# Denominators from a channel of ones, transposed weights on SyncE's queue, and stores, filter writes and mixing on GpSimd, in a two-layer attention and spectral-filter kernel

## The chip, the cores and the metric

The kernel runs on one core of one Trainium2 chip. The metric is device time in microseconds (us) of one launch. A core has five engines that each work through their own list of instructions in order: TensorE (PE; its weight loads are listed as PEld), VectorE (DVE), ScalarE (ACT), GpSimd (POOL) and SyncE (SP). Transfers (DMAs) are issued by SP, ACT or POOL.

## The reference

The input x has the shape (2, 128, 64, 64). Layer 0 is a group norm and a block with 7x7 neighbourhood attention in 4 heads; the change touches only its last piece, which makes the tokens. Layer 1 works on 4096 tokens of 128 channels per batch:

```python
t = _to_tokens(x)
t = t + _L1_attn_ref(_ln_t(t))      # softmax(q q^T / sqrt(128)), diagonal masked, times q
t = t + _L1_ffn_ref(_ln_t(t), sigma, phi, M_u, M_phi_plus, M_phi_minus, log_weights, gumbel)
x = _from_tokens(t, x)
```

`_ln_t` is a layer norm without scale or shift, so the 128 channels of every token `q` sum to zero. `_L1_ffn_ref` is a causal convolution over the sequence with 16 filters `phi`, once on `u` and once on `u` with alternating signs; each filter has its own 128x128 matrices `M_phi_plus[i, k]` and `M_phi_minus[i, k]`, scaled by `sigma ** 0.25`. To it come three lags `M_u[i]`. There are four branches `i`, with sequences of 4096, 2048, 1024 and 512 tokens, summed with the weights of a hard choice over four values. The kernel computes with mixed matrices, the sum over the branches of weight times matrix.

## The kernel before

Three stages follow one another in time. From 0 to about 347 us layer 0 runs in an order written out by hand. From there to about 1341 us the attention of layer 1 runs, batch 0 and then batch 1, with smaller work laid between its steps. From 1341 us to the end the convolution runs as bursts and projections on 32-row tiles (L1511, L1530), which read what the attention stage wrote to DRAM. In the attention stage the kernel emits instructions pair by pair and a scheduler sets each engine's order.

**Attention.** A batch is 8 chunks of 512 tokens. Because q q^T is symmetric, only the 36 pairs (a, c) with a <= c are scored: `weights` makes a quarter of a pair, a matmul of the channel-major tokens `cm` (L923, L933), then `exp` on ScalarE (L928, L940), whose `accum_out` also adds up a row's sum into `part`. Four quarters of a pair are four steps. In every step one matmul adds to `other`, the rows of chunk c (L1052), and others to `own`, the rows of chunk a, which needs the transposed weights (L987). For 27 of the 36 pairs, the far ones, the transpose goes by DRAM: `sent` writes the 128x2048 weights to `eb` from ScalarE's queue (1 MB), `moved` reads them back into `et` by four DMAs that change places of 32-blocks (L961), and `turned` transposes inside the blocks on VectorE (two of L970) and sums them into `part` (L972). The constants `MOVE, TURN, DELAY = 2, 5, 6` say how many steps after the last quarter these are emitted, the last of them for the own matmuls. There are two `et` and four `eb` buffers. The pair (6, 7) is turned by TensorE (`turned_here`), the blocks on the diagonal by TensorE and VectorE (L946 to L948). The sums of `other` and `own` gather in `xa` (L992, L994, L1069, L1071).

**After a chunk.** When `own` of chunk a is whole, `complete` calls `fill`, which queues the generator `after`: it transposes `xa` (L1089), sums `part` and takes the reciprocal (L1091, L1092), adds the attention to the residual tokens `tt` (L1094), makes a layer norm (L183, L184 on VectorE, a power on GpSimd at L174, L191 on VectorE), transposes the result to `zc`, and computes the forward transform of the chunk for the convolution: matmuls with `tr`, then `store`, in which ScalarE copies half of a result from PSUM (L1115), VectorE adds and subtracts it into `ub` (L1118, four buffers) and SP writes `ub` to `us` in DRAM (L1122, L1127). An `after` issues 16 such DMAs. There are 16 `after`s, 8 in each batch. `yield True` ends a step of the queued work; a plain `yield` ends the turn of the generator too.

**Other work laid between.** `filters` computes the transformed filters from `phi_pad`, with GpSimd adds (L1326, L1337), and writes them to `gs` in DRAM by 32 SP DMAs (L1302). `tokens(1)` makes the tokens of batch 1. `mixed` loads the branches' matrices one after another into `st` (two buffers, SP, L1250), multiplies the first by its weight (L1253) and adds the others (L1255), on VectorE. `filter_matrices` calls it for 4 groups of 4 filters, plus and minus, and after each group makes sums and differences times `sg` (L1266 to L1271, `mdiff`); it runs between 963 and 1080 us, in batch 1. `short_lags` are the three lags (matmul L1180, L1196). After `filter_matrices`, `blocks` loads the first `ct` from `gs` (L1413).

**Start of the convolution.** Its first inputs `ut` (L1492) are read from `us` and wait until all of `us` is written.

The steps of a pair are passed on so:

```python
while coming_ and coming_[0][0] + MOVE <= step:
    at, eb, a, c = coming_.pop(0)
    et = moved(eb)
    turns.append((at + TURN, et, a, c))
    late.extend((at + DELAY, a, c, et, t) for t in range(4))
```

Of the kernel before, what the change touches and what calls it, by code (L numbers as in the profile page):

```python
# [14 lines left out]
P = 128  # L15
# [8 lines left out]
MASKED = -1.0e30  # L24
MOVE, TURN, DELAY = 2, 5, 6

# [76 lines left out]
def kernel(  # L103
# [100 lines left out]
    def token_tiles(b, n0, pt):  # L204
        for j in range(4):
# [7 lines left out]
            )  # L213

    def tokens(b, bank):

        for n0 in range(0, NT, 4):
            pt = bank()
            token_tiles(b, n0, pt)
            nc.scalar.copy(tt[b][:, n0 : n0 + 4, :].rearrange("p j c -> p (j c)"), pt)  # L220
            yield
            stats = ln_statistics(tt[b][:, n0 : n0 + 4, :])
            yield
            ln_apply(tok[b][:, n0 : n0 + 4, :], tt[b][:, n0 : n0 + 4, :], stats)
            yield
            pt = bank()
            transposed(pt, tok[b][:, n0 : n0 + 4, :])
            nc.scalar.copy(cm[b][:, n0 * P : (n0 + 4) * P], pt)
            yield

# [4 lines left out]
    with l0a:  # L235
# [489 lines left out]
        @piece("k.cm")  # L725
        def _(t, b, g):
            nc.scalar.copy(cm[0][:, t["n0"] * P : (t["n0"] + 4) * P], t["kb"])


# [141 lines left out]
    with ap_:  # L871
# [24 lines left out]
        def attention(b, fill):  # L896
# [9 lines left out]

            part = sp.tile([P, NT, 9], F32, tag="part", name="part", bufs=1)
            nc.gpsimd.memset(part[:, :, 8:9], 0.0)
            pairs = [(a, c) for a in range(8) for c in range(a, 8)]
# [3 lines left out]
            def weights(a, c, k, left, halves):  # L913

                n = 4 * CHUNKS[a] + k
                lo = k * P if a == c else 0
                ps = bank()
                if k == 0:
                    halves.append(ep.tile([P, 2048], F32, tag="e", name="e"))
                eh = halves[0]  # L920
                keys = cm[b][:, chunk(c)]
                if far(a, c):
                    nc.tensor.matmul(  # L923
                        ps.rearrange("p (q t j) -> p q t j", q=4, t=4), lhsT=cm[b][:, n * P : (n + 1) * P],
                        rhs=keys.rearrange("p (t q j) -> p q t j", t=4, q=4), start=True, stop=True,
                    )
                    e = eh.rearrange("p (q k r) -> p k q r", q=4, k=4)[:, k]
                    nc.scalar.activation(  # L928
                        e, ps.rearrange("p (q r) -> p q r", q=4), AF.Exp, bias=0.0, scale=ASCALE,
                        accum_out=part[:, n, c : c + 1],  # L930
                    )
                    return e
                nc.tensor.matmul(  # L933
                    ps[:, lo:], lhsT=cm[b][:, n * P : (n + 1) * P], rhs=keys[:, lo:], start=True, stop=True
                )
                if a == c:
                    ks = slice(k * P, (k + 1) * P)
                    nc.vector.tensor_tensor(ps[:, ks], ps[:, ks], ndiag, ALU.add)
                e = eh[:, k * 512 : (k + 1) * 512]
                nc.scalar.activation(  # L940
                    e[:, lo:], ps[:, lo:], AF.Exp, bias=0.0, scale=ASCALE, accum_out=part[:, n, c : c + 1]
                )
                if lo:
                    pt = bank()
                    for j in range(k):
                        nc.tensor.transpose(pt[:, j * P : (j + 1) * P], left[j][:, lo : lo + P], ident)  # L946
                    nc.vector.tensor_copy(e[:, 0:lo], pt[:, 0:lo])
                    nc.vector.tensor_reduce(part[:, n, 8:9], e[:, 0:lo], AX.X, ALU.add)  # L948
                return e
# [7 lines left out]
            def moved(eb):  # L957

                et = ep.tile([P, 4, 512], F32, tag="et", name="et", bufs=2)
                for q in range(4):  # L960
                    nc.gpsimd.dma_start(  # L961
                        out=et[32 * q : 32 * q + 32], in_=eb[:, q].rearrange("(h p) r -> p h r", h=4)
                    )
                return et

            def turned(et, a, c):

                for q in (0, 2):
                    flat = et[:, q : q + 2].rearrange("p q r -> p (q r)")
                    nc.vector.transpose(flat, flat)  # L970
                n0 = 4 * CHUNKS[c]
                nc.vector.tensor_reduce(  # L972
                    part[:, n0 : n0 + 4, a], et.rearrange("p q (k t i) -> p t (q k) i", k=4, t=4), AX.XY, ALU.add
                )

            def turned_here(et, es, a, c, m):
# [4 lines left out]
                n = 4 * CHUNKS[c] + m  # L981
                nc.scalar.activation(
                    et[:, m], pt, AF.Identity, bias=0.0, scale=1.0, accum_out=part[:, n, a : a + 1]
                )

            def onto(own, n, out_, e, first, last):
                nc.tensor.matmul(out_, lhsT=tok[b][:, n, :], rhs=e, start=first, stop=last, skip_group_check=True)  # L987

            def complete(a, own):
# [3 lines left out]
                else:  # L993
                    nc.vector.tensor_copy(xs, own)  # L994
                fill(CHUNKS[a], part)

# [23 lines left out]
            def pass_on(n):  # L1020

                while coming_ and coming_[0][0] + MOVE <= step:
                    at, eb, a, c = coming_.pop(0)
                    et = moved(eb)
                    turns.append((at + TURN, et, a, c))
                    late.extend((at + DELAY, a, c, et, t) for t in range(4))
                while turns and turns[0][0] <= step:
                    turned(*turns.pop(0)[1:])
                while n and late and late[0][0] <= step:
# [7 lines left out]
            for i, (a, c) in enumerate(pairs):  # L1037
# [6 lines left out]
                for j in range(4):  # L1044
# [11 lines left out]
                    if a != c and not far(a, c):  # L1056
                        if j == 0:
                            here = ep.tile([P, 4, 512], F32, tag="et", name="et", bufs=2)
                        turned_here(here, es, a, c, j)
                        late.append((step + 1, a, c, here, j))  # L1060
# [20 lines left out]

        def after(b, c, part):

            n0 = 4 * c
            par, hf = divmod(c, 4)
# [4 lines left out]
            rden = sp.tile([P, 4], F32, tag="rden", name="rden")  # L1090
            nc.vector.tensor_reduce(rden, part[:, n0 : n0 + 4, :], AX.X, ALU.add)  # L1091
            nc.vector.reciprocal(rden, rden)  # L1092
            for j in range(4):
                nc.vector.scalar_tensor_tensor(  # L1094
                    tt[b][:, n0 + j, :], pt[:, j * P : (j + 1) * P], rden[:, j : j + 1], tt[b][:, n0 + j, :],
                    ALU.mult, ALU.add,
                )
            yield
            borrowed = b == 1 and spare not in ([], [None])
            z = spare.pop() if borrowed else sp.tile([P, 4, P], F32, tag="z4", name="z4")  # L1100
            layernorm(z, tt[b][:, n0 : n0 + 4, :])
            yield
# [8 lines left out]
            def store(pu, n, r0, m, ri):  # L1111

                for s in range(2):
                    half = sp.tile([P, 256], F32, tag="uo", name="uo", bufs=2)
                    nc.scalar.copy(half[:, 0:n], pu[s][:, n : 2 * n])  # L1115
                    ub = sp.tile([P, 2, 256], F32, tag="ub", name="ub", bufs=4)
                    for sgn, op in enumerate((ALU.add, ALU.subtract)):
                        nc.vector.tensor_tensor(ub[:, sgn, 0:n], pu[s][:, 0:n], half[:, 0:n], op)  # L1118
                    for sgn in range(2):
                        to = us[r0 : r0 + m, sgn, :, 2 * hh + s, 2 * fp : 2 * fp + 2, b, par, :]  # L1120
                        if ri is not None:
                            nc.sync.dma_start(  # L1122
                                out=to[:, ri], in_=ub[:, sgn, :].rearrange("p (f d) -> p f d", d=P)
                            )
                            continue
                        for f in range(2):
                            nc.sync.dma_start(  # L1127
                                out=to[:, :, f].rearrange("k i d -> i k d"), in_=ub[64 * f : 64 * f + 64, sgn, 0:P]
# [116 lines left out]
        def mixed(dst, src):  # L1245
            dst2 = dst.rearrange("p k e -> p (k e)")
            for i in range(NBR):
# [26 lines left out]
        def filters():  # L1274
# [22 lines left out]
            def store(src, r0, n, ri, s, i, o):  # L1297
# [3 lines left out]
                )  # L1301
                nc.sync.dma_start(out=to, in_=src)  # L1302

# [43 lines left out]
        def filler(b, steps, kept=None):  # L1347

            urgent, done = [], []

            def fill(c=None, part=None):
                if c is not None:
                    done.append(c)
                    urgent.append(after(b, c, part))
                    if len(done) % 4 == 0:
# [446 lines left out]
```

## Time and profile before

| | value |
|---|---|
| median of 3 runs | 2115.12 us (2111.28 to 2119.82) |
| profiled execution | 2113.34 us |
| its span | 2111.6 us |
| granted TensorE clock, mean | 0.969 |
| DMA `et<-eb`, issue to landing | 5.6 us (median of 216) |
| `us<-ub` | 128 DMAs of 128 KB and 128 smaller ones |

The page names an instruction by its source line, engine, operation and tiles. Busy time is the sum of the durations of a group; the idle time beside it is the time the engine stood just before such an instruction, with what ended it. A wait that the page gives to one engine on another ends with the named instruction. All durations come from the one profiled execution; its span is 1.7 us shorter than its time. The windows cut the span into stretches and give each engine's busy time in them, with the number of its instructions.

### The profile page before, as it was taken

Reading aid. Unit: us, or ns where it says so; the run is one execution under the profiler, and the core shown is the slowest. Engines: PE = TensorE matmul, PEld = TensorE weight load, DVE = VectorE, ACT = ScalarE, POOL = GpSimd, SP = SyncE. Lnnn points to the kernel's source line nnn. Section 1 sums busy time; section 2 is a strip of 40 time slices with the busy share of each in tenths; the row PEclk is TensorE's granted clock in tenths of the full one; section 3 lists DMA queues with packets and bytes.
Section 4 is the critical chain, followed back from the end, with each engine's and each line's share of the span. In section 5 each row is a group of like instructions: output and inputs, shape, how many; then the busy total and the mean of one; then the engine's idle time right before and its main releaser. Section 6 shows DMA issues by size and latency. Waiting matters only on the chain.

```text
span 2111.6 us, 51431 instructions
## 1 busy us (share of the span) xinstructions
PE 1942.4 (92%) x20504; PEld 1356.1 (64%) x20504; DVE 1112.5 (53%) x3172; ACT 735.7 (35%) x1990; POOL 592.0 (28%) x996
## 2 busy tenths in 40 slices
PE   6899998977999999997689989899999999999998
PEld 4577775433444444443234444599999899999987
DVE  5799986644755565554665657433333334333332
ACT  3789985212233223222022222222222222222222
POOL 3367876424321111111111110022222112222211
PEclk9999999998999999998889999999999999999999
DMA  4222222565565542648665562222222123222211
GB/s 151 60 61 60 62 61 62 161 157 172 147 204 164 162 127 78 177 117 239 143 177 160 149 181 72 82 67 66 69 67 67 48 55 101 67 67 67 66 47 42
DMA packets 264558, 226.01 MB, mean 107 GB/s; under 512 B 122607, under 2 KB 241535, under 8 KB 256896
## 3 DMA queue, kind: packets, MB, share of 16 engines
q1 hardware_dynamic: 238338, 105.95, 18.7%
q0 software_dynamic: 17856, 58.73, 12.3%
q10 hardware_dynamic: 8126, 58.04, 6.9%
q8 instruction: 163, 2.67, 0.6%
q14 instruction: 75, 0.61, 0.1%
HBM read 131.40 MB, written 91.25 MB: 105 GB/s over the span
## 4 chain that ended last, share of the span: by engine, by line
PE 57%; DMA 9%; DVE 7%; POOL 2%; issue 2%; SPq 1%; ACT 1%; DVEq 0%; POOLq 0%; ACTq 0%
PE acc L1530 27%; PE own L987 8%; PE pc L1511 7%; PE other L1052 5%; PE bank L923 4%; DMA us<-ub 4%; DMA et<-eb 2%; PE bank L933 2%; DVE et L970 1%; DMA st<-in_m_minus_dram 1%; PE bank L202 1%; DMA st<-in_m_plus_dram 1%; PE bank L1180 1%; PE pc L1569 1%; POOL ln_rs L174 1%
## 5 line engine op out<-in xcount | busy, mean ns | idle before, releaser
L1516 DVE COPY y<-pc 128x512 f32<-128x512 f32 x320 | 206.2, 686 | 349.0 <-PE pc L1511 348.6
L1530 PE MATMUL acc<-y,mpl 32*128 32x256 f32 x5120 | 325.4, 380 | 0.8 <-DVE af L1540 0.8
L1530 PE MATMUL acc<-y,mmi 32*128 32x256 f32 x5120 | 316.5, 375 | 0.0
L1516 ACT COPY y<-pc 128x512 f32<-128x512 f32 x320 | 172.1, 589 | 397.2 <-PE pc L1511 380.6
L1530 PEld LDWEIGHTS acc<-y,mpl 32*128 32x128 f32 x5120 | 290.5, 186 | 8.2 <-DVE af L1540 1.3
L1530 PEld LDWEIGHTS acc<-y,mmi 32*128 32x128 f32 x5120 | 290.9, 185 | 3.9
L928 ACT ACTIVATE e<-bank 128x512 f32<-128x512 f32 x216 | 129.3, 599 | 411.9 <-PE bank L923 395.2
L1052 PE MATMUL other<-e,tok 128*128 128x512 f32 x448 | 232.4, 621 | 30.0 <-DVE xa L1069 13.3
L987 PE MATMUL own<-et,tok 128*128 128x512 f32 x448 | 213.7, 616 | 36.3 <-DVE et L970 36.1
L961 POOL DMA_DIRECT2D et<-eb x216 | 119.3, 558 | 415.4 <-DMA eb<-e 143.1
L923 PE MATMUL bank<-cm 128*128 128x512 f32 x432 | 222.8, 612 | 9.2 <-DVE ub L1118 8.9
L1511 PE MATMUL pc<-ct,ut 32*128 32x256 f32 x2560 | 213.1, 377 | 4.2 <-DMA ut<-us 2.3
L1541 POOL TENSOR_TENSOR af<-af 128x512 f32<-128x512 f32 x39 | 49.7, 1275 | 590.3 <-DVE af L1540 504.3
L987 PEld LDWEIGHTS own<-et,tok 128*128 128x128 f32 x448 | 86.5, 197 | 148.8 <-issue 98.5
L1511 PEld LDWEIGHTS pc<-ct,ut 32*128 32x128 f32 x2560 | 173.0, 186 | 10.4 <-DVE y L1516 3.9
L1052 PEld LDWEIGHTS other<-e,tok 128*128 128x128 f32 x448 | 84.1, 197 | 132.5 <-issue 112.5
L970 DVE STREAM_TRANSPOSE et<-et 128x1024 f32<-128x1024 f32 x108 | 128.0, 1220 | 27.3 <-DMA et<-eb 27.2
L923 PEld LDWEIGHTS bank<-cm 128*128 128x128 f32 x432 | 76.7, 195 | 84.3 <-issue 69.5
L972 DVE TENSOR_REDUCE part<-et 128x4 f32<-128x2048 f32 x54 | 123.2, 2282 | 1.1
L541 ACT ACTIVATE p<-p,mn 128x196 f32<-128x196 f32 x256 | 114.4, 449 | 12.9 <-DVE mn L531 12.3
L1118 DVE TENSOR_TENSOR ub<-bank,uo 128x256 f32<-128x256 f32 (+1 forms) x192 | 60.6, 372 | 110.5 <-DMA us<-ub 45.7
L174 POOL TENSOR_TENSOR ln_rs<-ln_rs,mhalf 128x4 f32<-128x4 f32 x24 | 24.7, 1030 | 289.5 <-DVE ln_rs L173 245.5
(264 smaller groups left out, 2672.5 us busy)
## 6 DMA issues: line engine op xcount, KB each, us to landing
eb<-e ACTq DMA_DIRECT2D x54, 1024.0 KB
et<-eb POOLq DMA_DIRECT2D x216, 256.0 KB, 5.6
ut<-us SPq DMA_DIRECT2D x160, 128.0 KB
us<-ub SPq DMA_DIRECT2D x128, 128.0 KB
ct<-gs SPq DMA_DIRECT2D x320, 40.0 KB
vw<-vd SPq DMA_DIRECT2D x256, 49.0 KB
ct<-gs SPq DMA_DIRECT2D x320, 32.0 KB
vd<-v SPq DMA_DIRECT2D x128, 32.0 KB
```

Source lines behind the costliest of these rows:

```text
L541: nc.scalar.activation(p, p, AF.Exp, bias=t[name + "mn"][:, h : h + 1], scale=-1.0, accum_out=t["den"][:, u, h : h + 1],)
L923: nc.tensor.matmul(ps.rearrange("p (q t j) -> p q t j", q=4, t=4), lhsT=cm[b][:, n * P : (n + 1) * P], rhs=keys.rearrange("p (t q j) -> p ...
L928: nc.scalar.activation(e, ps.rearrange("p (q r) -> p q r", q=4), AF.Exp, bias=0.0, scale=ASCALE, accum_out=part[:, n, c : c + 1],)
L961: nc.gpsimd.dma_start(out=et[32 * q : 32 * q + 32], in_=eb[:, q].rearrange("(h p) r -> p h r", h=4))
L970: nc.vector.transpose(flat, flat)
L972: nc.vector.tensor_reduce(part[:, n0 : n0 + 4, a], et.rearrange("p q (k t i) -> p t (q k) i", k=4, t=4), AX.XY, ALU.add)
L987: nc.tensor.matmul(out_, lhsT=tok[b][:, n, :], rhs=e, start=first, stop=last, skip_group_check=True)
L1052: nc.tensor.matmul(turn(other, "p (q r) -> p q r"), lhsT=tok[b][:, n, :], rhs=es[j], start=(j == 0), stop=(j == 3),)
L1118: nc.vector.tensor_tensor(ub[:, sgn, 0:n], pu[s][:, 0:n], half[:, 0:n], op)
L1511: nc.tensor.matmul(pcs[j].rearrange("p (g o c) -> p o g c", g=4, o=2)[:, :, at], lhsT=ut[rows_, par, :], rhs=cv_[rows_], start=True, stop= ...
L1516: (nc.scalar.copy if j % 2 else nc.vector.tensor_copy)(y[:, :, :, 4 * kl + j, :], pcs[j].rearrange("p (g x k) -> p k g x", g=4, k=KF))
L1530: nc.tensor.matmul(acc[j][:, 0:256], lhsT=(mmi if l else mpl)[rows_, k, :], rhs=y[rows_, k, 2 * l : 2 * l + 2].rearrange("p s n x -> p (s ...
```

## The change

1. Channel 127 of the value tokens `tok` is set to one after `cm` has been made (`count`), so channel 127 of `own` and `other` is the denominator. The sums into `part` (the `accum_out` of L928, L940, L982, the reductions L948, L972, L1091) are gone. `after` takes the reciprocal of channel 127 and rebuilds the true channel 127 as minus the sum of the other 127.
2. `MOVE, TURN, DELAY` become 3, 7, 8; the DMAs of `moved` are issued by SP; the transposes of `turned` and the own matmuls keep their program order. The copy of `turned_here` goes from ScalarE to VectorE.
3. `store`: ScalarE copies both halves of a result to SBUF, GpSimd adds and subtracts, and GpSimd issues the `us` DMAs.
4. The `gs` writes are issued by GpSimd.
5. `mixed` runs on GpSimd: a multiply in place and an add where there was one instruction.
6. `after` has two more `yield True`, at its start and between the statistics and the application of the layer norm.

```diff
-MOVE, TURN, DELAY = 2, 5, 6
+MOVE, TURN, DELAY = 3, 7, 8
...
+    def count(b, n0):
+        nc.gpsimd.memset(tok[b][:, n0 : n0 + 4, P - 1 : P], 1.0)
...
             nc.scalar.copy(cm[b][:, n0 * P : (n0 + 4) * P], pt)
+            count(b, n0)
...
             nc.scalar.copy(cm[0][:, t["n0"] * P : (t["n0"] + 4) * P], t["kb"])
+            count(0, t["n0"])
...
-            part = sp.tile([P, NT, 9], F32, tag="part", name="part", bufs=1)
-            nc.gpsimd.memset(part[:, :, 8:9], 0.0)
...
-                        e, ps.rearrange("p (q r) -> p q r", q=4), AF.Exp, bias=0.0, scale=ASCALE,
-                        accum_out=part[:, n, c : c + 1],
+                        e, ps.rearrange("p (q r) -> p q r", q=4), AF.Exp, bias=0.0, scale=ASCALE
...
-                nc.vector.tensor_reduce(part[:, n, 8:9], e[:, 0:lo], AX.X, ALU.add)
...
-                    nc.gpsimd.dma_start(
+                    nc.sync.dma_start(
                         out=et[32 * q : 32 * q + 32], in_=eb[:, q].rearrange("(h p) r -> p h r", h=4)
                     )
...
-            def turned(et, a, c):
+            def turned(et):
                 for q in (0, 2):
                     flat = et[:, q : q + 2].rearrange("p q r -> p (q r)")
-                    nc.vector.transpose(flat, flat)
-                n0 = 4 * CHUNKS[c]
-                nc.vector.tensor_reduce(
-                    part[:, n0 : n0 + 4, a], et.rearrange("p q (k t i) -> p t (q k) i", k=4, t=4), AX.XY, ALU.add
-                )
+                    tc.keep_in_program_order(nc.vector.transpose(flat, flat))
...
-                nc.scalar.activation(
-                    et[:, m], pt, AF.Identity, bias=0.0, scale=1.0, accum_out=part[:, n, a : a + 1]
-                )
+                nc.vector.tensor_copy(et[:, m], pt)
...
+                tc.keep_in_program_order(
+                    nc.tensor.matmul(out_, lhsT=tok[b][:, n, :], rhs=e, start=first, stop=last, skip_group_check=True)
+                )
-                nc.tensor.matmul(out_, lhsT=tok[b][:, n, :], rhs=e, start=first, stop=last, skip_group_check=True)
...
-        def after(b, c, part):
+        def after(b, c):
+            yield True
...
-            nc.vector.tensor_reduce(rden, part[:, n0 : n0 + 4, :], AX.X, ALU.add)
-            nc.vector.reciprocal(rden, rden)
+            kept_, out_ = tt[b][:, n0 : n0 + 4, :], pt.rearrange("p (j d) -> p j d", d=P)
+            nc.vector.reciprocal(rden, out_[:, :, P - 1])
+            rest = sp.tile([P, 4], F32, tag="rest", name="rest")
+            nc.vector.tensor_reduce(rest, out_[:, :, 0 : P - 1], AX.X, ALU.add)
             for j in range(4):
                 nc.vector.scalar_tensor_tensor(
-                    tt[b][:, n0 + j, :], pt[:, j * P : (j + 1) * P], rden[:, j : j + 1], tt[b][:, n0 + j, :],
+                    kept_[:, j, 0 : P - 1], out_[:, j, 0 : P - 1], rden[:, j : j + 1], kept_[:, j, 0 : P - 1],
                     ALU.mult, ALU.add,
                 )
+            nc.vector.tensor_tensor(rest, rest, rden, ALU.mult)
+            nc.vector.tensor_tensor(kept_[:, :, P - 1], kept_[:, :, P - 1], rest, ALU.subtract)
...
-            layernorm(z, tt[b][:, n0 : n0 + 4, :])
+            stats = ln_statistics(kept_)
+            yield True
+            ln_apply(z, kept_, stats)
...
-                    half = sp.tile([P, 256], F32, tag="uo", name="uo", bufs=2)
-                    nc.scalar.copy(half[:, 0:n], pu[s][:, n : 2 * n])
+                    both = sp.tile([P, 512], F32, tag="uo", name="uo", bufs=2)
+                    nc.scalar.copy(both[:, 0 : 2 * n], pu[s][:, 0 : 2 * n])
                     ub = sp.tile([P, 2, 256], F32, tag="ub", name="ub", bufs=4)
                     for sgn, op in enumerate((ALU.add, ALU.subtract)):
-                        nc.vector.tensor_tensor(ub[:, sgn, 0:n], pu[s][:, 0:n], half[:, 0:n], op)
+                        nc.gpsimd.tensor_tensor(ub[:, sgn, 0:n], both[:, 0:n], both[:, n : 2 * n], op)
...
-                            nc.sync.dma_start(
+                            nc.gpsimd.dma_start(
                                 out=to[:, ri], in_=ub[:, sgn, :].rearrange("p (f d) -> p f d", d=P)
...
-                            nc.sync.dma_start(
+                            nc.gpsimd.dma_start(
                                 out=to[:, :, f].rearrange("k i d -> i k d"), in_=ub[64 * f : 64 * f + 64, sgn, 0:P]
...
-                    nc.vector.tensor_scalar(dst2, st2, wt[:, 0:1], None, ALU.mult)
+                    nc.gpsimd.tensor_scalar(dst2, st2, wt[:, 0:1], None, ALU.mult)
                 else:
-                    nc.vector.scalar_tensor_tensor(dst2, st2, wt[:, i : i + 1], dst2, ALU.mult, ALU.add)
+                    nc.gpsimd.tensor_scalar(st2, st2, wt[:, i : i + 1], None, ALU.mult)
+                    nc.gpsimd.tensor_tensor(dst2, dst2, st2, ALU.add)
...
-                nc.sync.dma_start(out=to, in_=src)
+                nc.gpsimd.dma_start(out=to, in_=src)
```

More of the change, by code (lines that the diff above doesn't have):

```diff
@@ L940, in weights @@
                 nc.scalar.activation(
-                    e[:, lo:], ps[:, lo:], AF.Exp, bias=0.0, scale=ASCALE, accum_out=part[:, n, c : c + 1]
+                    e[:, lo:], ps[:, lo:], AF.Exp, bias=0.0, scale=ASCALE
                 )
@@ L964, in moved, with turned_here @@
                 return et
-            def turned(et, a, c):
+            def turned(et):
                 for q in (0, 2):
                     flat = et[:, q : q + 2].rearrange("p q r -> p (q r)")
-                    nc.vector.transpose(flat, flat)
-                n0 = 4 * CHUNKS[c]
-                nc.vector.tensor_reduce(
-                    part[:, n0 : n0 + 4, a], et.rearrange("p q (k t i) -> p t (q k) i", k=4, t=4), AX.XY, ALU.add
-                )
-            def turned_here(et, es, a, c, m):
+                    tc.keep_in_program_order(nc.vector.transpose(flat, flat))
+            def turned_here(et, es, m):
                 pt = bank()
@@ L980, in turned_here, with onto @@
                     nc.tensor.transpose(pt[:, k * P : (k + 1) * P], es[k][:, m * P : (m + 1) * P], ident)
-                n = 4 * CHUNKS[c] + m
-                nc.scalar.activation(
-                    et[:, m], pt, AF.Identity, bias=0.0, scale=1.0, accum_out=part[:, n, a : a + 1]
-                )
-            def onto(own, n, out_, e, first, last):
-                nc.tensor.matmul(out_, lhsT=tok[b][:, n, :], rhs=e, start=first, stop=last, skip_group_check=True)
+                nc.vector.tensor_copy(et[:, m], pt)
+            def onto(own, n, out_, e, first, last):
+                tc.keep_in_program_order(
+                    nc.tensor.matmul(out_, lhsT=tok[b][:, n, :], rhs=e, start=first, stop=last, skip_group_check=True)
+                )
             def complete(a, own):
@@ L994, in complete @@
                     nc.vector.tensor_copy(xs, own)
-                fill(CHUNKS[a], part)
+                fill(CHUNKS[a])
             def pair_onto(own, a, c, et, t):
@@ L1024, in pass_on @@
                     et = moved(eb)
-                    turns.append((at + TURN, et, a, c))
+                    turns.append((at + TURN, et))
                     late.extend((at + DELAY, a, c, et, t) for t in range(4))
                 while turns and turns[0][0] <= step:
-                    turned(*turns.pop(0)[1:])
+                    turned(turns.pop(0)[1])
                 while n and late and late[0][0] <= step:
@@ L1058, in attention @@
                             here = ep.tile([P, 4, 512], F32, tag="et", name="et", bufs=2)
-                        turned_here(here, es, a, c, j)
+                        turned_here(here, es, j)
                         late.append((step + 1, a, c, here, j))
@@ L1349, in filler, with fill @@
             urgent, done = [], []
-            def fill(c=None, part=None):
+            def fill(c=None):
                 if c is not None:
                     done.append(c)
-                    urgent.append(after(b, c, part))
+                    urgent.append(after(b, c))
                     if len(done) % 4 == 0:
```

## The prediction

> **What bounds the kernel now.** I read the page's shares and slices first, then busy time by stage, then what TensorE waits for, then the cost groups, and last the timeline of the last stores. The shares, and two rows of the slices:
>
> ```profile
> PE 1942.4 (92%) x20504; PEld 1356.1 (64%) x20504; DVE 1112.5 (53%) x3172; ACT 735.7 (35%) x1990; POOL 592.0 (28%) x996
> ...
> POOL 3367876424321111111111110022222112222211
> PEclk9999999998999999998889999999999999999999
> ```
>
> TensorE is busy 92% of the span; no other engine is over 53%. A slice is 2111.6/40 = 52.8 us. POOL stands at one tenth through slices 13 to 24, the attention: it has room. The same by stage (columns: window, length, busy us and count of PE, PEld, DVE, ACT, POOL, clock, DMA share, GB/s):
>
> ```profile
> 600.00:700.00 100.00, 95.06 (x277) 43.29 (x276) 62.79 (x121) 27.72 (x82) 20.48 (x34) 1.00 0.60 172
> ...
> 1000.00:1100.00 100.00, 70.10 (x172) 29.99 (x173) 66.67 (x128) 15.09 (x45) 11.95 (x21) 0.83 0.62 165
> ...
> 1350.00:2112.00 762.00, 746.49 (x13236) 722.04 (x13232) 260.45 (x464) 210.99 (x424) 165.75 (x390) 0.99 0.24 64
> ```
>
> The last 762 us, the spectral stage, have TensorE full and are not touched. The edits lie in 347 to 1341 us. There the windows give idle PE time of 59.7 us (347 to 950), 40.6 us (963 to 1080, where the filters of the branches are mixed, clock 0.81), 16.3 us (1080 to 1297) and 5.1 us (1297 to 1341). What PE waited for in 347 to 1341 (total, times, longest):
>
> ```profile
> PE own L987 <- DVE et L970: 36.1, 12, 12.8
> PE other L1052 <- DVE xa L1069: 13.3, 7, 7.4
> PE other L1052 <- DVE rden L1092: 9.1, 1, 9.1
> PE bank L923 <- DVE ub L1118: 8.9, 5, 3.9
> ...
> PE bank L946 <- DVE ub L1118: 7.4, 2, 3.9
> PE bank L1315 <- DVE ub L1118: 5.4, 1, 5.4
> ...
> PE bank L202 <- DVE ub L1118: 4.4, 2, 2.3
> ```
>
> So VectorE is named nearly always, though it is little over half busy: it works in order, and stands at one instruction while others are ready. Which instruction, the groups say (busy, mean ns | idle before, releaser):
>
> ```profile
> L961 POOL DMA_DIRECT2D et<-eb x216 | 119.3, 558 | 415.4 <-DMA eb<-e 143.1
> L1541 POOL TENSOR_TENSOR af<-af 128x512 f32<-128x512 f32 x39 | 49.7, 1275 | 590.3 <-DVE af L1540 504.3
> ...
> L970 DVE STREAM_TRANSPOSE et<-et 128x1024 f32<-128x1024 f32 x108 | 128.0, 1220 | 27.3 <-DMA et<-eb 27.2
> L972 DVE TENSOR_REDUCE part<-et 128x4 f32<-128x2048 f32 x54 | 123.2, 2282 | 1.1
> L1118 DVE TENSOR_TENSOR ub<-bank,uo 128x256 f32<-128x256 f32 (+1 forms) x192 | 60.6, 372 | 110.5 <-DMA us<-ub 45.7
> ```
>
> VectorE idles 110 us ahead of the stores' adds (L1118), 45.7 of it until a `us` transfer has given a `ub` buffer back. The end of the stage on SP's queue:
>
> ```profile
> 1326.03 4.09 SPq L1122 DMA_DIRECT2D us<-ub  x8
> 1330.21 4.43 SPq L1127 DMA_DIRECT2D us<-ub  x8
> 1338.65 2.24 SPq L1492 DMA_DIRECT2D ut<-us  x5
> ```
>
> The spectral stage's first load waits until every `us` store has landed, 4 us after the last issue: the stores of the last `after` are on the path.
>
> **What the Trainium skill says.** "GPSIMD Engine Reference", Performance versus the Vector engine: an elementwise add of two tensors takes GpSimd about twice as long as VectorE (1.96). The trace agrees: 1275 ns against 685 (L1069) at 128x512. "DMA: Bandwidth & Descriptors", Anatomy of one DMA: a semaphore wait of a transfer is held on the issuing sequencer. The trace agrees: POOL's `et` issues waited 143.1 us for `eb`; after the change SP waits so, with all behind it. The same page, Issuing engines are not separate DMA queues: another issuer saves sequencer time only. I take it so: `et` keeps its 5.6 us to land. The same page, SWDGE vs HWDGE vs iDMA: GpSimd computes descriptors in software. How long it takes for `us` stores in 512-byte runs no row shows; 558 ns for an `et` DMA in 2 KB runs is the nearest.
>
> **Part 1, the denominators.** Gone from VectorE: L972 123.2, L948 48 x 0.41 = 19.7, L1091 2.9 us. Added: one reduce of 128x508 an `after`, 16 x 0.6 = 10 (L972 is 1.1 ns an element), 32 tiny ones at 0.17 = 5, the turned copies of pair (6,7), 8 x 0.69 = 5.5. ScalarE loses 56 us of accumulator reads (42.0 and 14.1), which were not on the path. The memsets, 16 at some 0.2 us, lie in idle POOL.
>
> **Part 2, the way of `et`.** POOL loses 119.3 us of issue, SP gains them. After the score e leaves, `eb` takes 9 us, four issues 2.2, landing 5.6, two transposes 2.4: 19 us unhindered, up to 23 in the chain. A step is a quarter of a pair, 288 in both batches; PE's 859 busy us between 347 and 1341 make it 3.0 us. DELAY was 6 steps = 18 us, late by 1 to 5; with 8 it is 24. The two `et` buffers are held from step 3 to 12, 9 steps, where two buffers and a pair every 4 steps give 8: so `moved` also waits for the own matmuls of the pair two before, which end in step 3; some 5 steps = 15 us are left for the 10.2 of issue, landing and turn. That fits while SP has nothing else ahead; what does stand behind SP's wait there, `st` and `ct` loads, counts in part 5.
>
> **Part 3, the stores on POOL.** One `after` costs there 8 x 0.723 (L1326, 128x256) + 4 x 0.452 (L1546, 128x128) + 16 x 0.55 = 16.4 us; 16 of them 262 us. At twice the descriptor work of an issue (0.84) it would be 21; below 0.45, SP's fastest, nothing speaks for it: 15. VectorE loses 60.6 us, and above all the standing for `us`. ScalarE's copies grow from 0.34 to 0.60: 64 x 0.26 = 17 us beside PE. POOL meets `ub` itself: four buffers at 2.55 us are 10.2 us, over the 7.5 a `us` store takes, so it hardly stands. Behind a block of stores POOL holds the next layernorm's power (L174), and with it VectorE's z and PE's z transposes, by up to 16 us. The `after`s lie 35, 20 and 22 us apart at the batch boundary: 16.4 fits, and PE has scores to do meanwhile.
>
> **The gain of parts 1 to 3** outside mixing and end: the four `ub` waits 26.1; of L970's 36.1 the 9.7 outside 963 to 1080 (26.4 inside); of the waits for xa, z and tok (some 20 outside mixing) I credit 9, since VectorE's queue is shorter. The rden wait (9.1) stays: VectorE stands there for a filter load. 45 us. Bounds: 26 if only `ub` goes; 65 if most of the 76 us of idle goes with clock recovered.
>
> **Part 4, gs.** 32 issues x 0.55 = 18 us on POOL, between its own adds there: the filter stage has POOL 47 us; nothing to +8, I take 4.
>
> **Part 5, mixing on POOL.** Eight blocks of four loads, in pairs. VectorE did a load in 0.75 us, waiting 2.9 to 7 for it. POOL: 1.5 (128x512 by a scalar, L647 to L1337: 1.49 to 1.57) for the first, 1.5 + 1.28 for each other: 2 x 1.5 + 6 x 2.8 = 19.7 us a group, and with two `st` buffers and 3.4 us a load, walked by hand, 27.4 for the first group and 29.7 for each other: 117 us. Beside the 20 `ct` loads that share SP, 125 to 130. What hangs on it: in the program's order on VectorE the turns of pairs 11, 12, 13 of batch 1 follow the second, third and fourth mdiff (which need POOL's result), and on SP the `et` loads of pair 13 stand behind the 31st `st` load, which waits for POOL to free `st`. PE's own matmuls of 11 to 13 wait on all that. Before, from the stage's first z transposes (951.5) to the end of pair 13's own (1071.6) were 120 us. After: 13 + 127 + 10 = 150, less 4 of work that PE does in it: +26. Bounds: +5 (loads overlap fully, 4 x 19.7 = 79, PE then bound as before) and +50.
>
> **Part 6, the end.** Three `after`s come at 1297.7, 1302 and 1306. POOL issues in the order stores 6, power 7, stores 7, power 8, stores 8 (L174 is 1.0 us, and 4.4 us from the power's start through z, transposes and matmul to the next store). So 3 x 16.4 + 2 x 4.4 + 4 landing = 62 us from 1297.7, where before it was 40.7: +21; and those stores start about 7 us later against PE's work, as POOL still serves the one before: +28. Cover: lag matmuls (L1180) only, which PE has done by then. Bounds +12 and +40.
>
> **Sum.** -45 + 4 + 26 + 28 = +13 us on the profiled 2113.3: 2126. The median of the runs shown is 1.8 over the profiled time: 2128.
>
> **Rivals.** *Faster: VectorE's relief is worth more and the new prices hide.* For: VectorE is named in nearly all waits of PE; POOL's mean load after is only 450 of 994 us. Against: both prices stand in one engine's order. -55 + 5 + 10 = -40: 2075. *Much slower: GpSimd decides.* One mechanism: it builds descriptors for 512-byte runs at 0.84 us or more, from where an `after` takes 21 us, over the 20 to 22 of the boundary. The end is +14 more, mixing and boundary +13: 2155. For: no `us` store was ever issued there; against: 558 ns for a DMA of twice the bytes. *No change:* the gain is at 50 and end and mixing at 45 to 50 together: 2113. That the change doesn't do what it says: the order shows every part moved, so only the worth is open.
>
> **How the numbers follow.** Forecast 0.42 (2112 to 2145), faster 0.34, much slower 0.19, no change 0.05. A measurement of this kernel tells about 0.5% (10.6 us) from no change. A third of the forecast's case and most of no change lie within it: same 0.17; slower 0.28 + 0.19 = 0.47; faster 0.36. Range 2060 to 2160, from the faster case with 65 us of gain to the much slower one; the forecast's own is 2112 to 2145.
>
> **What would show it.** Right: no ub line of DVE among PE's waits; in the stretch of mixing POOL busy over 80 us with `st` loads as its releaser, PE idle over 50; at the end three blocks of `us` issues on POOL of 9 us or more, ut<-us 15 us or more later after the third-last store's start than 41. Wrong: the stretch of mixing under 120 us, or the end under 50; a `us` issue on POOL far from 0.55; or PE idle in 347 to 950 still over 45, which would say that VectorE's queue was not its cause.

## The result and the profile after

The changed kernel takes 2125.7 us (median of 6 runs, 2123.4 to 2126.6), the kernel before 2114.2 us (6 runs, 2108.6 to 2119.8): a ratio of 1.0054, interval 1.0036 to 1.0071. The profiled execution took 2125.07 us, its span is 2123.1 us, the mean clock 0.954 where it was 0.969. The little difference hides three large ones. First the page of the changed kernel, its shares and two rows of slices:

```profile
PE 1936.9 (91%) x20504; PEld 1359.2 (64%) x20504; DVE 915.9 (43%) x2882; ACT 724.1 (34%) x1686; POOL 874.7 (41%) x1337
...
POOL 3377877239143347146733337322222112222211
PEclk8999998998999999998599996899999999999999
```

VectorE has lost 197 us of work and GpSimd has gained 283. The row of clocks has two dips, in slices 20 and 25 (1008 to 1062 us and 1274 to 1327 us), where TensorE stood. What PE waited for in 347 to 1355 us (total, times, longest):

```profile
PE own L983 <- DVE et L972: 48.5, 6, 39.8
PE bank L202 <- DVE z L191: 35.6, 9, 16.9
PE own L983 <- DMA et<-eb: 17.2, 1, 17.2
PE bank L202 <- POOL tok L720: 7.1, 4, 6.1
```

The waits for `ub`, four rows and 26.1 us before, are gone. Few long waits stand in place of the many short ones: 39.8 us and 17.2 us in the mixing, 26.9 us of the second row at the end, 6.1 us at the start. The groups on GpSimd (busy, mean ns | idle before):

```profile
L1122 POOL TENSOR_TENSOR ub<-uo 128x256 f32<-128x256 f32 (+1 forms) x192 | 118.6, 644 | 81.7 <-ACT uo L1119 80.1
...
L1126 POOL DMA_DIRECT2D us<-ub x128 | 93.8, 734 | 0.0
```

Both kernels do the same pairs in the same order, so the moments at which a chunk's sum `own` is added to `xa` (L992 and L994 before, L989 and L991 after, start in us) make a ledger of the stages:

| moment | before | after | after - before | change in the stage |
|---|---|---|---|---|
| first sum of `other` (L1071, L1068) | 368.8 | 377.4 | +8.6 | +8.6 |
| chunk 0 of batch 1 whole | 944.3 | 916.0 | -28.3 | -36.9 |
| chunk 1 of batch 1 whole (the mixing lies between) | 1071.7 | 1070.0 | -1.7 | +26.6 |
| last chunk whole | 1306.5 | 1278.0 | -28.5 | -26.8 |
| first burst matmul | 1341.1 | 1350.7 | +9.6 | +38.1 |
| end of the span | 2111.6 | 2123.1 | +11.5 | +1.9 |

Attention itself became 63.7 us shorter; the start, the mixing and the end gave back 73.3.

In the mixing VectorE's timeline of the changed kernel (start, duration, instruction, idle time before it and its end) shows who stood for whom:

```profile
1004.44 0.69 DVE L1271 TENSOR_TENSOR mdiff<-mpl,mmi 128x512 f32<-128x512 f32 x1 [9.39 <-POOL mmi L1260]
...
1009.24 2.37 DVE L972 STREAM_TRANSPOSE et<-et 128x1024 f32<-128x1024 f32 x2 [1.69 <-DMA et<-eb]
...
1031.51 0.69 DVE L1271 TENSOR_TENSOR mdiff<-mpl,mmi 128x512 f32<-128x512 f32 x1 [16.20 <-POOL mmi L1260]
...
1034.56 2.36 DVE L972 STREAM_TRANSPOSE et<-et 128x1024 f32<-128x1024 f32 x2
```

TensorE's own matmuls resumed at 1036.97, at the end of the second turn, after 39.83 us:

```profile
1036.97 9.43 PE L983 MATMUL own<-et,tok 128*128 128x512 f32 x16 [39.83 <-DVE et L972]
```

They need the turn of pair 11 first (the numbers count the far pairs of a batch), and VectorE made the turns of pairs 11 and 12 in exchanged places. SP issued the last `et` load of pair 11 and of pair 12 here:

```profile
978.71 0.50 SPq L963 DMA_DIRECT2D et<-eb  x1
...
1004.85 0.50 SPq L963 DMA_DIRECT2D et<-eb  x1
```

The turn at 1009.24 still stood 1.69 us for a load, so it is that of pair 12, whose last load was issued 4.4 us before. Pair 11 was turned at 1034.56, behind a difference for which GpSimd had to add until 1031.5. The change marks both turns to keep their program order; why they changed places all the same is not known.

At the end of the stage GpSimd's timeline shows the three blocks, here the borders of the last two:

```profile
1296.58 1.04 POOL L174 TENSOR_TENSOR ln_rs<-ln_rs,mhalf 128x4 f32<-128x4 f32 x1
1302.52 1.41 POOL L1122 TENSOR_TENSOR ub<-uo 128x256 f32<-128x256 f32 x2 [4.90 <-ACT uo L1119]
...
1320.86 1.04 POOL L174 TENSOR_TENSOR ln_rs<-ln_rs,mhalf 128x4 f32<-128x4 f32 x1
1326.36 1.41 POOL L1122 TENSOR_TENSOR ub<-uo 128x256 f32<-128x256 f32 x2 [4.46 <-ACT uo L1119]
...
1343.25 1.97 POOL L1131 DMA_DIRECT2D us<-ub  x3 [0.55 <-issue]
```

The power of the next chunk's layer norm starts when the block of stores before it is through: its input was ready at 1287.7 and at 1311.8 (VectorE's L173), 9 us earlier each time. The last `us` store was issued at 1345, and SP's first `ut` load at 1348.25.

### The profile page after: what moved, and what is told of

It is laid out like the page before. It is cut to its first block, busy times and chain, and to the rows that moved or that the text cites. A ratio compares the mean times of both kernels' runs of the same rounds, so it can differ in the third digit from the quotient of the medians.

```text
span 2123.1 us, 50883 instructions
## 1 busy us (share of the span) xinstructions
PE 1936.9 (91%) x20504; PEld 1359.2 (64%) x20504; DVE 915.9 (43%) x2882; ACT 724.1 (34%) x1686; POOL 874.7 (41%) x1337
## 4 chain that ended last, share of the span: by engine, by line
PE 43%; POOL 3%; DVE 2%; issue 2%; DMA 1%; SPq 0%; ACT 0%; DVEq 0%; POOLq 0%; ACTq 0%
PE acc L1535 26%; PE pc L1516 7%; PE own L983 3%; PE other L1049 2%; PE bank L927 2%; POOL ub L1122 1%; PE pc L1574 1%; PE bank L936 1%; POOL us L1131 1%; POOL us L1126 1%; PE pc L1587 0%; PE bank L1141 0%; DMA et<-eb 0%; PE pc L1616 0%; POOL st L1259 0%
## 5 line engine op out<-in xcount | busy, mean ns | idle before, releaser
L1122 POOL TENSOR_TENSOR ub<-uo 128x256 f32<-128x256 f32 (+1 forms) x192 | 118.6, 644 | 81.7 <-ACT uo L1119 80.1
L972 DVE STREAM_TRANSPOSE et<-et 128x1024 f32<-128x1024 f32 x108 | 127.7, 1221 | 38.3 <-DMA et<-eb 37.2
L1126 POOL DMA_DIRECT2D us<-ub x128 | 93.8, 734 | 0.0
L1119 ACT COPY uo<-bank 128x512 f32<-128x512 f32 (+1 forms) x96 | 47.5, 516 | 122.2 <-POOL ub L1122 53.5
```

The lines of the kernel that those rows point to most:

```text
L972: tc.keep_in_program_order(nc.vector.transpose(flat, flat))
L1122: nc.gpsimd.tensor_tensor(ub[:, sgn, 0:n], both[:, 0:n], both[:, n : 2 * n], op)
L1126: nc.gpsimd.dma_start(out=to[:, ri], in_=ub[:, sgn, :].rearrange("p (f d) -> p f d", d=P))
```

## The experiments

Each edit is made to the changed kernel, or to an experiment that is named. Times are medians; the ratio is to the kernel before, measured again beside each group of runs (medians 2111.7 to 2114.7 us), with its interval. The stages are those of the ledger, from one profiled execution each. Executions of one kernel differ by up to 11 us (a_both 2045.8 to 2056.0, c_stores 2062.5 to 2073.4), and the stretch to chunk 0 differs by 2 us between the changed kernel and a_late, which have the same code there: stage differences of a few us say nothing.

| run | us | ratio (interval) | to chunk 0 of batch 1 | mixing | to last chunk | end |
|---|---|---|---|---|---|---|
| before | 2114.2 | 1 | 944.3 | 127.4 | 234.8 | 34.6 |
| changed | 2125.7 | 1.0054 (1.0036 to 1.0071) | 916.0 | 154.0 | 208.0 | 72.7 |
| a_mix | 2081.1 | 0.9845 (0.9827 to 0.9862) | 901.0 | 123.4 | 208.0 | 72.5 |
| a_late | 2091.6 | 0.9897 (0.9879 to 0.9914) | 913.9 | 153.7 | 208.8 | 42.3 |
| a_both | 2050.7 | 0.9702 (0.9678 to 0.9726) | 905.8 | 126.3 | 208.8 | 41.6 |
| a_ussp | 2098.5 | 0.9930 (0.9909 to 0.9951) | 919.1 | 152.8 | 210.9 | 43.9 |
| a_mu | 2115.4 | 1.0009 (0.9999 to 1.0019) | 904.4 | 153.9 | 208.0 | 72.7 |
| d_mdiff | 2120.5 | 1.0037 (1.0023 to 1.0051) | 913.4 | 129.5 | 231.2 | 72.6 |
| d_stpool | 2155.2 | 1.0192 (1.0113 to 1.0272) | 916.3 | 185.3 | 208.0 | 72.8 |
| c_stores | 2067.8 | 0.9798 (0.9779 to 0.9817) | 906.9 | 130.1 | 212.2 | 41.1 |
| c_den | 2086.0 | 0.9872 (0.9849 to 0.9896) | 920.5 | 137.6 | 217.2 | 38.9 |
| c_et | 2137.6 | 1.0115 (1.0100 to 1.0130) | 959.5 | 130.3 | 227.9 | 42.1 |
| c_steps | 2093.3 | 0.9910 (0.9882 to 0.9937) | 935.2 | 113.6 | 228.1 | 42.2 |
| c_etst | 2096.1 | 0.9908 (0.9879 to 0.9937) | 931.0 | 128.4 | 221.6 | 42.2 |

### The two prices: mixing and end

a_mix puts the arithmetic of `mixed` back:

```diff
-                    nc.gpsimd.tensor_scalar(dst2, st2, wt[:, 0:1], None, ALU.mult)
+                    nc.vector.tensor_scalar(dst2, st2, wt[:, 0:1], None, ALU.mult)
                 else:
-                    nc.gpsimd.tensor_scalar(st2, st2, wt[:, i : i + 1], None, ALU.mult)
-                    nc.gpsimd.tensor_tensor(dst2, dst2, st2, ALU.add)
+                    nc.vector.scalar_tensor_tensor(dst2, st2, wt[:, i : i + 1], dst2, ALU.mult, ALU.add)
```

> The changed kernel with the arithmetic of the mixing back on VectorE, all else as changed. Theory 1 (GpSimd's two instructions a load, with VectorE's mdiff and the turns waiting for them, are the price): the stretch from complete(0) to complete(1) of batch 1, 154 us in the changed kernel, goes back to 120 to 130, and the 8.6 us lost at the first tokens (GpSimd mixed m_u ahead of the last layer norms) come back: 2125.7 - 27 - 8 = about 2090. Rival (the et loads that stand behind st loads on SyncE are the price, whoever adds): the stretch stays over 140, the total over 2110.

It gained 44.7 us, more than expected. The mixing went from 154.0 to 123.4, and chunk 0 of batch 1 was whole 15.0 us earlier. The rival fails: SP's order of `et` behind `st` was left as it was.

a_late treats the stores of three chunks as before:

```diff
+LATE = (3, 6, 7)
...
-                    nc.scalar.copy(both[:, 0 : 2 * n], pu[s][:, 0 : 2 * n])
+                    late_ = b == 1 and c in LATE
+                    lo_ = n if late_ else 0
+                    nc.scalar.copy(both[:, lo_ : 2 * n], pu[s][:, lo_ : 2 * n])
...
+                    issue = nc.sync if late_ else nc.gpsimd
...
+                        if late_:
+                            nc.vector.tensor_tensor(ub[:, sgn, 0:n], pu[s][:, 0:n], both[:, n : 2 * n], op)
...
```

> The changed kernel with the stores of the last three chunks of batch 1 (3, 6, 7) as before: VectorE adds, SyncE issues. Theory 1 (three blocks of 18.6 us of stores in one queue set the end): from the last own sum to the first burst 72.7 us become 35 to 45, total about 2093 to 2100. Rival (transposes, lag matmuls and the landing set the end; in the kernel before it took 34.6 us because the stores had begun earlier): no more than 15 us, total over 2110.

The end fell by 30.4 us and the total by 34.1. a_both makes both edits:

> Both edits together. Theory 1: the two prices lie one after the other and add: about 2060 to 2068, 2 to 2.5% under the kernel before. Rival (one hides the other, or the freed time is lost to the filter matrices' loads): over 2085.

It takes 2050.7 us, 3.0% less than the kernel before, and better than expected: the two gains are 44.7 + 34.1 = 78.8 us alone and 75.0 together. They lie one after the other. On its page TensorE's share is up, and VectorE has 165 us less than before:

```profile
PE 1926.4 (94%) x20504; PEld 1354.7 (66%) x20504; DVE 948.0 (46%) x2954; ACT 719.7 (35%) x1686; POOL 731.4 (36%) x1190
```

a_ussp leaves every addition on GpSimd and gives the issuing of `us` to SP (two lines, `nc.gpsimd.dma_start` to `nc.sync.dma_start`).

> The changed kernel with GpSimd still adding but SyncE issuing all us stores. Theory 1: GpSimd's block per chunk falls from 18.6 to 7.4 us, so the end loses 15 to 25 us; against it SyncE stands for the adds with et loads behind, some 5 us: total 2105 to 2115. Rival (SyncE's waits for us hold up et, as the in-order queue would have it): the stretches of attention grow by more than the end gains, total 2125 or more.

The end fell by 28.8 us, nearly as much as in a_late, and the total by 27.2, more than expected. So the issues in GpSimd's order set the end (0.73 and 0.67 us each, 11.3 us of a block of 18.9), and not the additions alone. The rival fails: the stretches to chunk 0 and to the last chunk grew by 3.1 and 2.9 us, near the 5 us expected of SP's standing for the additions but hardly more than the scatter.

a_mu gives only the first mixing, that of `m_u` at 354 us, back to VectorE:

```diff
-            mixed(mu, m_u)
+            mixed(mu, m_u, nc.vector)
...
```

> The changed kernel with only the mixing of m_u (4 loads, 8.5 us of GpSimd at 354 us, ahead of the last tokens' power and scaling) back on VectorE. Theory 1: the first other sum comes 8 to 9 us earlier and the total falls by 8 to 14, to 2112 to 2118; a_mix's 44.7 us then are some 31 in the mixing of batch 1 and the rest here. Rival (the loss there is made up by the next wait): total within 4 us of the changed kernel.

It gained 10.3 us, and the first sum of `other` came at 365.6 instead of 377.4. In the changed kernel GpSimd multiplied and added `m_u` from 353.8 to 362.3 us, and the last power and scaling of the layer-0 tokens stood behind it; PE stood 6.15 us for them and its next matmuls ran at a granted clock of 0.50 (windows 363 to 368 and 368 to 372 us).

### What the price of the mixing is made of

d_mdiff moves the sums and scalings of `filter_matrices` to GpSimd too (`nc.vector` to `nc.gpsimd` in four lines).

> The changed kernel with the sums and scalings after each mixed group (mdiff) on GpSimd as well, so that VectorE never stands for GpSimd there; GpSimd gets about 36 us more work, SyncE's order of st and et stays. Theory 2a (the turns behind mdiff on VectorE are the price): the stretch complete(0) to complete(1) falls from 154 to 135 or less although GpSimd works longer. Theory 2b (et loads behind st loads on SyncE are): it grows to 165 or more.

The mixing fell to 129.5 although GpSimd did more: VectorE's standing at `mdiff`, with the exchange of the turns, was most of the price. The total fell by only 5.2 us, because GpSimd was late for the next layer norm and its stores. PE's waits in 1043 to 1135 us of this run:

```profile
PE bank L202 <- DVE z L191: 20.4, 3, 18.8
```

The stretch to the last chunk was 231.2 instead of 208.0. In this kernel the turns also kept their places; they are exchanged in the changed kernel, a_late, a_ussp, a_mu and d_stpool, the five whose VectorE waits for GpSimd at `mdiff`: there the own matmuls of both pairs begin only after the second turn. Standing and exchange went together in every run, and were not tried apart. An estimate from the changed kernel makes the exchange the smaller part: with the same two moments of turning in the other order, half of the 16 own matmuls, some 5 us of their 9.43, could have run after 1011.6, and the other half still only from 1036.9.

d_stpool has GpSimd issue the `st` loads itself (`nc.sync` to `nc.gpsimd` in one line).

> The changed kernel with the st loads issued by GpSimd itself, so that SyncE's et loads have nothing of the mixing ahead; the loads cost GpSimd 32 issues, some 20 us, and VectorE still stands at mdiff. Theory 2a (VectorE at mdiff): the stretch stays at 145 or more. Theory 2b (SyncE's order): it falls to 135 or less.

The mixing grew to 185.3: with nothing of the mixing left on SP, the price did not fall. GpSimd's 32 issues took it 25.3 us, and its own waits for `st` are 33.2 us where they were 29.7, so this run shows that SP's order isn't the main price, and not that it costs nothing.

### What the gain is made of

These go out from a_both. c_stores puts all stores back on VectorE and SP (`late_ = True`).

> a_both with every store, of both batches, as before: VectorE adds, SyncE issues. It prices part 3 outside the end. Theory 1 (the gain is VectorE no longer standing for us transfers, worth 26 us of named waits): 2050.7 + 20 to 30 = 2070 to 2080, and DVE ub waits of PE come back. Rival (the gain is from the denominators, whose reductions are 143 us of VectorE's time; the stores are cheap once VectorE's queue is short): within 8 us of a_both.

It lost 17.1 us, between the two theories, and PE's waits for `ub` did not come back at all. VectorE's own wait for `us` transfers, 45.7 us before, was now

```profile
DVE ub L1127 <- DMA us<-ub: 1.6, 2, 1.4
```

So something other than moving the stores had ended that standing.

c_den undoes part 1 as well (`accum_out`, L948, L972 and the sum of `part` restored; `count` left out; `uo` 256 wide as before).

> c_stores with the denominators by accumulation as before (part 1 undone too): only the SyncE et loads, the longer delay, gs on GpSimd and the new yields are left of the change. Against c_stores it prices part 1. Theory 1 (VectorE's length is not the bound, its standing is): plus 8 to 20. Rival (the 143 us of reductions are the gain): plus 30 or more, at or over the kernel before.

It lost 18.2 us more, within theory 1, and is still 1.3% faster than the kernel before. What is left of the change in it is part 2 (but for the copy of `turned_here`), `gs` on GpSimd and the new yields. Although its stores are on VectorE and SP, the waits for `ub` (PE's) and for `us` transfers (VectorE's) hardly came back here either, in 347 to 1341 us:

```profile
PE bank L1154 <- DVE ub L1133: 1.9, 2, 0.9
...
DVE ub L1133 <- DMA us<-ub: 0.4, 1, 0.4
```

c_et undoes part 2 in a_both, the kept program order included:

```diff
-MOVE, TURN, DELAY = 3, 7, 8
+MOVE, TURN, DELAY = 2, 5, 6
...
-                    nc.sync.dma_start(
+                    nc.gpsimd.dma_start(
                         out=et[32 * q : 32 * q + 32], in_=eb[:, q].rearrange("(h p) r -> p h r", h=4)
...
```

> a_both with part 2 undone: the et loads on GpSimd, 2, 5, 6 steps, no kept order. Theory 1 (part 2 is worth the 9.7 us of turned waits outside the mixing, and on GpSimd the et issues would now stand behind 18.6 us blocks of stores): plus 20 to 60, 2070 to 2110. Rival (SyncE and the longer delay bring nothing): within 8 us.

It lost 86.9 us, more than expected, and is slower than the kernel before. Two runs part the steps from the queue. c_steps changes only the first line:

> a_both with MOVE, TURN, DELAY back at 2, 5, 6, the et loads staying on SyncE. It parts what undoing part 2 cost in c_et (87 us) into the steps and the queue. Theory 3a (the collision of et issues with GpSimd's blocks of stores was most of it): here plus 15 to 40, about 2065 to 2090. Theory 3b (the steps, 18 us where the way of et takes 19 to 23, are most of it): plus 60 or more, over 2110.

c_etst is c_et with `late_ = True`, so that GpSimd issues `et` without blocks of stores:

> c_et with all stores on VectorE and SyncE, so that GpSimd issues et with little ahead of it; steps 2, 5, 6. Theory 3a (collision on GpSimd): 2095 or less, 40 us under c_et although VectorE has the stores again. Theory 3b: within 20 us of c_et or over it.

c_steps lost 42.6 us, a little more than theory 3a had; c_etst is 41.5 us faster than c_et, as 3a had. Undoing part 2 costs about half by the steps, half by `et` issues in a queue with stores; the kept order is given up in c_et and c_etst and not in c_steps, and its share was not tried alone. With the stores on VectorE the parts add almost exactly: part 1 takes the kernel before to c_etst (2113.2 to 2096.1, -17.1, with parts 4 and 6) or c_den to c_stores (-18.2); part 2 takes c_etst to c_stores (-28.3) or the kernel before to c_den (-27.6, with 4 and 6). Parts 4 and 6 leave nothing over that these runs could tell (their intervals are some 5 us to either side). Part 2 is what makes part 3 pay: the stores on GpSimd gain 17.1 us with it (c_stores to a_both) and lose 41.5 us without it (c_etst to c_et).

## Why the prediction was right

The forecast was 2128 us, the measurement 2125.7. The direction was right and the two large costs were paid where they had been named, but that the total came within 3 us was luck: the gain was taken too small by 18.7 us, and the prices by nearly as much. The terms are these.

- **What bounds the kernel.** Right in part: VectorE, not full but standing, held TensorE. PE was idle 32.8 us in 347 to 923 after, 59.7 us in about the same work before (347 to 950). But what relieved VectorE (parts 1 and 3) brought 35 us of the gain, and the way of `et` (part 2) the other 28.
- **The gain.** Taken as 45 us (26 to 65), measured 63.7 by the ledger; the chain of runs to the version without the two prices gives 63.5 (before to c_den 28.2, c_den to c_stores 18.2, c_stores to a_both 17.1, against 2114.2). The sum was too small, and its division wrong. I credited 26.1 us of `ub` waits to the stores' move, but c_den still has the stores on VectorE and SP and 1.9 us of these waits: the rest went with the edits that c_den keeps, and which of these ended them (part 2, the yields or `gs`) was not tried. Part 2 was credited with 9.7 us and brought 28: PE's named waits for `et` had shown only part of what it was worth.
- **Mixing on GpSimd.** Taken as +26, measured +26.6 in that stretch. GpSimd's own pace was as worked out: from 940.8 to 1058.1 us, 117 us, at 1.56 and 1.26 us an instruction. The mechanism was half shown: VectorE at `mdiff`, with the exchange, was most of the price (d_mdiff, 154.0 to 129.5), while SP's order is not shown as a price of its own. The profile puts the last wait, 17.2 us for pair 13, down to its `et` loads, issued behind the last `st` loads at 1048 to 1054; but VectorE's fourth difference began at 1058.13, just as GpSimd's last addition ended (1058.09), and the turn followed that block at 1061.15 with no idle time between. The order is 12, 11, 13 and not 11, 12, 13 as the prediction put it. The 120 us taken for this stretch before are 121.8, since its first transposes ran at 949.88 and not at 951.5. The part missed was the other place of the same edit: `m_u`, +8.6 us at the start, 10.3 us in a_mu.
- **The end.** Taken as +28 (12 to 40), measured +38.1 by the ledger, 34.1 by a_late. The mechanism was right, block for block. The mis-sized terms are the issue, 0.734 us for a 128 KB `us` store and 0.673 us for a small one, where 0.55 was taken, so a block is 18.9 us (1277.68 to 1296.56) and not 16.4, and the way from a power's start to the next store, 5.9 and 5.5 us where 4.4 was taken. The issues lie between the 0.55 taken and the 0.84 of the stated higher case. From the first store of the three to the first `ut` load are 70.6 us, 62 were expected (before they were 40.9, and not 40.7).
- **gs.** Taken as +4 and not isolated; parts 4 and 6 together show nothing above the runs' scatter.

In sum -63.7 + 8.6 + 26.6 + 38.1 + 1.9 = +11.5, where the text had -45 + 4 + 26 + 28 = +13. The Trainium skill's ratio ("GPSIMD Engine Reference", Performance versus the Vector engine) nearly held for additions of two tensors: 1.26 us against 0.69 us at 128x512, 1.8 times, where the page has 1.96. Of the signs named beforehand, all those of being right came: no `ub` line of VectorE among PE's waits, GpSimd busy 86.4 us and PE idle 60.0 in 940 to 1058, three long blocks of issues, 70.6 us to the first `ut` load. Of those of being wrong, one came in part: the issue was a third above 0.55 for the large stores and a fifth above it for the small ones.

The faster rival was not far: had the mixing stayed on VectorE and the last stores too, its 2075 us would have been passed (a_both, 2050.7). It named both costs and took them as mostly hidden; in the changed kernel they were not, since they stood in order ahead of what TensorE needed next.

## What to carry to other kernels

Work moved to an engine with room is paid where a burst of it stands ahead of something short that another engine needs: price every place where the edit runs, at its start, middle and end, and count the instructions that come behind. A queue that has to be empty before the next stage begins should not hold the slow stores of the last chunks, even where its mean load is low. And a bundle whose total is zero may hold a gain: part it by stage before it is dropped.

## What the runs showed of the hardware

- The price of issuing a DMA from GpSimd did not go with its bytes: 0.558 us for 256 KB in runs of 2 KB (`et`, before), but 0.734 us for 128 KB in runs of 512 bytes and 0.673 us for 32 KB in such runs (`us`). From SP the last two blocks of 8 of the same stores in the kernel before took 4.09 and 4.43 us, 0.51 and 0.55 us each. An `st` load of 256 KB in 512 runs of 512 bytes took GpSimd 0.79 us (d_stpool). Among these DMAs in runs of 512 bytes the price rose with their number (64, 256 and 512 runs: 0.67, 0.73 and 0.79 us), far less than in proportion; the 128 longer runs of `et` cost less than any of them. What sets the price was not tried further.
- A multiply by a per-partition scalar on GpSimd took 1.56 us at 128x512, longer than an addition of two tensors there (1.26 us), and 3.2 times VectorE's 0.48 us.
- After TensorE had stood, its granted clock was lower. The Trainium skill describes a clock that is halved after TensorE has been idle ("TensorE: Matmul & The Clock Gate", Part 1: The HAM clock gate); the window in which the 6.15 us of standing at the start of the changed kernel end, and the one after it, agree with 0.50. In the two long stretches of standing the mean granted clock was 0.61 and 0.65, and single records of own matmuls took up to 1220 ns where the median is 592. The columns are length, busy PE, PEld, DVE, ACT, POOL, clock, DMA share, GB/s:

```profile
363.00:368.00 5.00, 2.44 (x5) 1.16 (x6) 0.00 (x0) 0.00 (x0) 4.81 (x7) 0.50 0.48 27
368.00:372.00 4.00, 4.00 (x6) 1.69 (x5) 2.43 (x12) 2.44 (x5) 1.32 (x3) 0.50 0.34 145
...
990.00:1040.00 50.00, 9.30 (x19) 3.73 (x18) 12.76 (x29) 1.19 (x2) 33.92 (x24) 0.61 0.47 130
1290.00:1350.00 60.00, 26.52 (x110) 14.80 (x110) 12.75 (x41) 10.21 (x18) 44.49 (x68) 0.65 0.20 52
```
